# Layer 1's bias goes into the kept x in DRAM, and the layer's end has one sum per tile

## The chip, the cores and the metric

The kernel runs on one core of a Trainium2 chip. The metric is device time in microseconds (us) of one execution, given as the median of the runs; less is better. Before the change it is 2073.58 us (three runs, 2071.27 to 2076.43).

## The reference

Four graph layers stand in a row on one graph of 2708 nodes with 512 features. Each begins with a layer norm and a ReLU, and each adds its result to x. Layer 1, the one that changes, is the only one with a plain bias and no ReLU after its weights:

```python
h = jnp.maximum(_layernorm(x, axis=-1), 0.0)
x = x + _L1_gnn_ref(h, adj, L1_gnn_W, L1_gnn_b)

def _L1_gnn_ref(x, adj, W, b):
    deg = adj.sum(axis=1)
    dis = (deg + EPS) ** (-0.5)
    a_norm = dis[:, None] * adj * dis[None, :]
    h = a_norm @ x
    return h @ W.T + b
```

Layers 0 and 2 end in `relu(aug @ h @ W)` with their own scaling of the adjacency, and layer 3 is two attention-like sums and a sigmoid. All values are float32.

## The kernel before

The 2708 nodes are cut into 22 tiles of up to 128 rows (tiles 0 to 19 are full, 20 and 21 hold the leftovers of the four quarters of the graph). The normalized features `h` of all tiles stay in SBUF. The running x does not: tile t is kept in DRAM as `xs[t]`, 128 by 512 floats, 256 KB.

A layer has two kinds of work.

1. *Products* (`aggregate`). The adjacency times h is done by a two-level scheme of seven products in place of eight. `aggregate` (L668) runs seven outer products in the order 1, 7, 2, 4, 6, 5, 3; each has two column halves u of seven inner products of ten matmuls (L541). For each half SyncE loads four adjacency blocks of 847.5 KB (L445 straight from the input, L447 from sums kept in DRAM) into seven places `obuf`, and VectorE makes the combinations t1, t2, t4 and t3 of them (L512, L513, L514, L516). VectorE also takes the products out of PSUM (L581, L588, L557 to L566). `hooks` may name a function that is traced right after an outer product.
2. *Ends* (`epilogue`, that is `next_x`, L919). Tiles 0 to 9 (H1) are ended before the last outer product 3, tiles 10 to 21 (H2) after it. For each tile: load the kept x (`load_x`, L914, issued by GpSimd, L916); project the aggregated tile through the weights on TensorE (L203, PSUM result `po`); in layer 1 VectorE forms `y = po * dis + b1` (L931), adds y to x (L934); GpSimd stores the new x to `xs[t]` (L935); VectorE takes mean and variance (L234, L235). For every group of three tiles the factors of the norm follow (L224 to L247) and ScalarE writes the new h (L255). In layers 0 and 2 ScalarE makes y with a ReLU in the place of L931. `po` has two PSUM banks, x has seven places, y two.

The bias b1 is fetched once, spread over the 128 partitions, into the place `misc[:, 0:D]` (L963).

The program is traced in order of its text. A planner then orders the instructions of each engine by a simulated time: an instruction stands in its engine's queue where its inputs and its place came free in that simulation, not where the text has it. Inside layer 0 part of the order is written out by hand (`tc.issue_after`); from layer 1 on it isn't. On the chip each queue runs strictly in its order, and all transfers of GpSimd are in one such queue with the waits before them.

Of the kernel before, what the change touches and what calls it, by code (L numbers as in the profile page):

```python
# [10 lines left out]
ALU = mybir.AluOpType  # L11

P = 128
D = 512
# [23 lines left out]
def gnn_kernel(  # L38
# [20 lines left out]
    nc = tc.nc  # L59
# [33 lines left out]
    dinv = dd[:, 1]  # L93
    dis = dd[:, 2]
# [7 lines left out]
    xs = [dram.tile([P, D], FP, name=f"xs{t}") for t in range(NT)]  # L102
# [35 lines left out]
    misc, ends_o = ends[:, ends_o : ends_o + 4 * D], ends_o + 4 * D  # L138
# [7 lines left out]
    def take(places):  # L146

        places.append(places.pop(0))
        return places[-1]

    def new_y():
        return take(y_places)

    def load_w(w):
        w_sb = w_place[:, 0 : NC * D].rearrange("p (c o) -> p c o", c=NC)
        nc.gpsimd.dma_start(w_sb, w.rearrange("(c p) o -> p c o", p=P))
        return w_sb
# [74 lines left out]
    def stats(src, mv):  # L232
        st = small.tile([P, nc.vector.BN_STATS_DIM], FP, tag="st", name="st")
        nc.vector.bn_stats(st, src)  # L234
        nc.vector.bn_aggr(mv, st)  # L235

    def rstd_of(mv, n):
        v = small_cols("rv", n)
        nc.vector.tensor_scalar(v[:, :n], mv[:, :n, 1], LN_EPS, None, ALU.add)
        rstd = small_cols("rstd", n)  # L240
        rsqrt(rstd[:, :n], v[:, :n], n)
        return rstd

    def shift_of(mv, scale, n, at=None):

        b = small_cols("sh", n)
        last = nc.vector.scalar_tensor_tensor(  # L247
            b[:, :n], mv[:, :n, 0], -1.0, scale[:, :n], ALU.mult, ALU.mult
        )
        if at is not None:  # L250
            at.append(last.ins)
        return b

    def normalized(t, src, scale, shift, fs=slice(0, D)):
        nc.scalar.activation(h[:, t, fs], src[:, fs], AF.Relu, bias=shift, scale=scale)  # L255

    def groups(ts):

        res = []
        for t in ts:  # L260
            if res and len(res[-1]) < GT:
                res[-1].append(t)
            else:
                res.append([t])
        return res
# [201 lines left out]
    def by_halves(f, *xs):  # L467

        for ts in (slice(0, KT), slice(KT, 2 * KT)):
            f(*(x[:, ts] for x in xs))  # L470

    def minus_sum(o, a, b):
        nc.vector.scalar_tensor_tensor(o, a, -1.0, b, ALU.mult, ALU.subtract)  # L473
# [45 lines left out]
    def outer_product(p, self_loops, *dests, at=None):  # L519

        X, key, times = OUTER[p]
        with tc.issue_after(at) if at is not None else nullcontext():
            xs_ = inner_x(X)
        if key in PLAIN:
            loops = times if self_loops else 0
        else:
            loops = 0 if self_loops else -times
        for u in range(U):
            blks = [load_o(key, a, b, u) for a, b in QUAD]
            with tc.issue_after(at) if at is not None else nullcontext():  # L530
                ys = inner_y(blks, u, loops)
            multiply(xs_, ys, u, dests)
            free.extend(blks)
# [101 lines left out]
    def tails(self_loops, qs, loaded=None):  # L635


        at = at_pe[-1]
        for n, q in enumerate(qs):
            blk, pieces = loaded[n] if loaded else tail_rows(self_loops, q)  # L640
            for u in range(U):
                tl = pieces[u]
                ps = [
                    (ps_agg if c < NC - 1 else ps_out).tile(
                        [P, W], FP, tag="agg" if c < NC - 1 else "out", name="pt"
                    )
                    for c in range(NC)
                ]
                with tc.issue_after(at) if loaded else nullcontext():
                    tail_products(ps, tl, True)  # L650
                for c in range(NC):
                    d = agg[:, c // 2, q // 2, c % 2, q % 2, u * W : (u + 1) * W]
                    at_end.append(nc.vector.tensor_add(d, d, ps[c]).ins)
            if blk is not None:
                free.append(blk)

    H1 = list(range(0, half))
    H2 = list(range(half, NT))


    def first_part_of_both():
        nc.scalar.copy(agg[:, 0, 1], agg[:, 0, 0])

    def ends_of_sums():
        nc.vector.tensor_add(agg[:, 1, 1], agg[:, 1, 1], agg[:, 0, 1])
        nc.vector.tensor_add(agg[:, 1, 0], agg[:, 1, 0], agg[:, 1, 1])

    def aggregate(self_loops, epilogue, hooks=None):  # L668


        def outer(p, *dests):
            outer_product(p, self_loops, *dests)
            if hooks is not None and p in hooks:
                hooks[p]()

        outer(1, (0, 0, "as it is"))
        first_part_of_both()
        by_halves(nc.vector.tensor_sub, XA, XA, XB)
        outer(7, (1, 1, "as it is"))
        nc.vector.tensor_sub(XB, XB, XD)  # L680
        outer(2, (0, 0, "added"))
        minus_sum(XA, XD, XA)
        nc.vector.tensor_add(XC, XC, XA)
        outer(4, (1, 0, "as it is"))
        tails(self_loops, (0, 1))
        outer(6, (0, 1, "added"))
        ends_of_sums()
        outer(5, (0, 1, "less"), (1, 1, "less"))
        tails(self_loops, (2, 3))
        epilogue(H1)  # L690
        outer(3, (0, 1, "added"))
        epilogue(H2)
# [218 lines left out]
    def project(w_sb, t):  # L911
        return tile_product(t, tile_cols(agg, t), [w_sb[:, c, :] for c in range(NC)])

    def load_x(t, src):  # L914
        xt = take(xt_places)
        nc.gpsimd.dma_start(xt, src[t])  # L916
        return xt

    def next_x(ts, w_sb, scale, bias, src, colscale, after=None):  # L919
        for g in groups(ts):  # L920
            n, t0 = len(g), g[0]
            mv = small.tile([P, KT, 2], FP, tag="mv", name="mv")
            xts = []
            for s, t in enumerate(g):
                xt = load_x(t, src)
                po = project(w_sb, t)
                y = new_y()
                if bias is None:
                    nc.scalar.activation(y, po, AF.Relu, scale=scale[:, t : t + 1])
                else:  # L930
                    nc.vector.scalar_tensor_tensor(  # L931
                        y, po, scale[:, t : t + 1], bias, ALU.mult, ALU.add
                    )
                nc.vector.tensor_add(xt, xt, y)  # L934
                nc.gpsimd.dma_start(xs[t], xt)  # L935
                stats(xt, mv[:, s, :])
                xts.append(xt)
            rstd = rstd_of(mv, n)
            if colscale is not None:
                nc.vector.tensor_mul(rstd[:, :n], rstd[:, :n], colscale[:, t0 : t0 + n])  # L940
            sh = shift_of(mv, rstd, n)
            for s, t in enumerate(g):
                normalized(t, xts[s], rstd[:, s : s + 1], sh[:, s : s + 1])
                if after is not None:
                    after(t)
# [5 lines left out]
    w_sb = []  # L951

    def first_epilogue(ts):
        if not w_sb:
            w_sb.append(load_w(w0))
        next_x(ts, w_sb[0], dinv, None, x, dis)

    first_aggregate(first_epilogue)


    w1_sb = load_w(w1)
    b1_bc = misc[:, 0:D]
    nc.gpsimd.dma_start(b1_bc, b1.partition_broadcast(P))  # L963
    aggregate(False, lambda ts: next_x(ts, w1_sb, dis, b1_bc, xs, dinv))


    def broadcast_columns(po, cs):
# [32 lines left out]
    def h_dots(ts):  # L1000
        for t in ts:
            for k in range(4):
                y = new_y()
                nc.vector.tensor_tensor_reduce(  # L1004
                    y, h[:, t, :], vs[:, k, :], 1.0, 0.0, ALU.mult, ALU.add, hd[:, t, k : k + 1]
                )
            nc.vector.tensor_add(hd[:, t, 2:4], hd[:, t, 2:4], bab)
            nc.vector.tensor_scalar(hd[:, t, 2:4], hd[:, t, 2:4], 0.5, None, ALU.mult)
# [10 lines left out]
    w2_sb = load_w(w2)  # L1019
    vs = None  # L1020

    def make_vs():
# [2 lines left out]

    aggregate(
        True,
        lambda ts: next_x(ts, w2_sb, dinv, None, xs, None, keep_h),
        {2: make_vs, 3: lambda: h_dots((5, 6))},
    )  # L1030

# [442 lines left out]
```

## Time and profile before

The page shows one profiled execution, of 2070.74 us by its own time; the program's instructions span 2069.0 us of it.

| what | us |
|---|---|
| median of the runs | 2073.58 |
| profiled execution | 2070.74 |
| its span | 2069.0 |
| layer 1's first product begins | 450.36 |
| layer 1, end of H1: first and last L931 | 721.03, 752.34 |
| layer 1, end of H2: first and last L931 | 795.36, 834.63 |
| L931, mean of 22 | 0.75 |
| L934 in layer 1, mean of 22 | 0.69 |

Times are from the start of the span. "Idle before, releaser" in a row tells how long the engine waited for that instruction and for what. For a transfer, the time to landing runs from its issue to the last byte's notice.

### The profile page before, as it was taken

How to read it: one execution, taken by the hardware profiler on the slowest of the kernel's cores; microseconds unless marked ns; L12 is line 12 of the kernel's file. 1: busy time of each engine (PE TensorE's matmuls, PEld its weight loads, DVE VectorE, ACT ScalarE, POOL GpSimd, SP SyncE). 2: the span in 40 equal slices, each digit the busy share in tenths (PEclk: the TensorE clock that was granted, in tenths of full speed). 3: DMA queues.
4: the chain of work that ended last, by engine and by line, in shares of the span. 5: the costliest groups of instructions: out<-in, count | busy, mean ns of one | idle time of the engine just before them, and what ended most of it. 6: DMA issues, size and time to landing. Idle time of an engine off the chain costs nothing.

```text
span 2069.0 us, 20285 instructions
## 1 busy us (share of the span) xinstructions
PE 2028.0 (98%) x7330; PEld 1282.2 (62%) x7330; DVE 1495.6 (72%) x2592; ACT 406.2 (20%) x822; POOL 198.8 (10%) x361
## 2 busy tenths in 40 slices
PE   5999999999999999999999999999999999999998
PEld 2566655646666655666664646666677666676666
DVE  4678877756777777766587889967758866677644
ACT  1430001130000010100002130000026444444411
POOL 0111111120000011100002130001001000001011
PEclk9999999999999999999999999999999999999999
DMA  9998595555545444754454565545543332323231
GB/s 369 305 378 265 180 338 187 190 186 179 174 154 176 146 168 142 239 178 161 161 170 144 204 208 188 171 156 186 185 147 121 112 105 95 110 88 123 87 100 52
DMA packets 81476, 363.69 MB, mean 176 GB/s; under 512 B 11568, under 2 KB 16876, under 8 KB 81248
## 3 DMA queue, kind: packets, MB, share of 16 engines
q1 hardware_dynamic: 51104, 245.95, 34.7%
q0 software_dynamic: 30272, 116.45, 17.4%
q8 instruction: 58, 0.95, 0.2%
q14 instruction: 42, 0.34, 0.0%
HBM read 297.39 MB, written 62.19 MB: 174 GB/s over the span
## 4 chain that ended last, share of the span: by engine, by line
PE 83%; DVE 7%; DMA 5%; issue 4%; POOL 1%; ACT 0%; SPq 0%; POOLq 0%; DVEq 0%; ACTq 0%
PE pe L1364 17%; PE pc L541 13%; PE pa L541 13%; PE pd L541 13%; PE po L203 8%; PE pb L541 7%; PE pt L603 3%; DMA obuf<-in_yb_dram 3%; PE pd L1077 1%; PE pc L1077 1%; PE pa L1077 1%; PE pt L608 1%; PE pe L603 1%; DMA osumt<-ends 1%; DVE ends L1004 1%
## 5 line engine op out<-in xcount | busy, mean ns | idle before, releaser
L1364 PE MATMUL pe<-obuf,h 128*128 128x339 f32 x1280 | 373.2, 448 | 0.0
L541 PE MATMUL pa<-obuf,h 128*128 128x339 f32 x1040 | 317.0, 449 | 2.5 <-ACT h L255 1.4
L1364 PEld LDWEIGHTS pe<-obuf,h 128*128 128x128 f32 x1280 | 241.4, 189 | 121.8 <-issue 4.1
L541 PEld LDWEIGHTS pa<-obuf,h 128*128 128x128 f32 x1040 | 195.2, 189 | 109.5 <-issue 9.2
L203 PE MATMUL po<-ends,agg 128*128 128x512 f32 x480 | 207.5, 593 | 0.0
L1228 ACT ACTIVATE e<-r,nsr 128x339 f32<-128x339 f32 x352 | 172.4, 566 | 178.5 <-DVE obuf L1232 86.4
L541 PE MATMUL pb<-t,s 128*128 128x339 f32 x560 | 170.9, 451 | 1.8 <-DVE s L473 1.0
L541 PE MATMUL pc<-t,h 128*128 128x339 f32 x560 | 169.5, 448 | 1.5 <-DVE u L588 1.5
L541 PE MATMUL pd<-t,s 128*128 128x339 f32 x560 | 169.0, 447 | 0.0
L541 PE MATMUL pd<-obuf,s 128*128 128x339 f32 x550 | 166.3, 448 | 0.2 <-DVE agg L562 0.2
L575 ACT COPY v<-pa 128x339 f32<-128x339 f32 x56 | 24.6, 439 | 718.2 <-PE pa L541 691.3
L203 PEld LDWEIGHTS po<-ends,agg 128*128 128x128 f32 x480 | 90.9, 190 | 114.3 <-issue 109.3
L541 PEld LDWEIGHTS pb<-t,s 128*128 128x128 f32 x560 | 106.3, 191 | 57.3 <-DVE t L513 2.1
L541 PEld LDWEIGHTS pc<-t,h 128*128 128x128 f32 x560 | 105.7, 189 | 56.8 <-DVE u L588 3.1
L541 PEld LDWEIGHTS pd<-t,s 128*128 128x128 f32 x560 | 105.8, 189 | 54.1
L541 PEld LDWEIGHTS pd<-obuf,s 128*128 128x128 f32 x550 | 104.0, 189 | 53.9 <-DVE agg L562 1.3
L541 PE MATMUL pc<-obuf,s 128*128 128x339 f32 x450 | 135.9, 448 | 0.0
L541 PEld LDWEIGHTS pc<-obuf,s 128*128 128x128 f32 x450 | 85.1, 189 | 43.8 <-issue 0.5
L935 POOL DMA_DIRECT2D xs<-ends x66 | 35.9, 544 | 780.6 <-DVE ends L934 705.4
L513 DVE TENSOR_TENSOR t<-obuf,t 128x1695 f32<-128x1695 f32 x55 | 105.3, 1915 | 0.0
L1232 DVE SCALAR_TENSOR_TENSOR obuf<-obuf,e 128x1695 f32<-128x1695 f32 x32 | 61.5, 1923 | 57.9 <-DMA obuf<-in_yb_dram 40.7
L514 DVE TENSOR_TENSOR t<-obuf,t 128x1695 f32<-128x1695 f32 x52 | 99.5, 1914 | 0.1
(321 smaller groups left out, 2415.4 us busy)
## 6 DMA issues: line engine op xcount, KB each, us to landing
obuf<-in_yb_dram SPq DMA_DIRECT2D x132, 847.5 KB, 4.5
obuf<-osumt SPq DMA_DIRECT2D x100, 847.5 KB, 4.5
osumt<-obuf POOLq DMA_DIRECT2D x22, 847.5 KB, 12.2
xs<-ends POOLq DMA_DIRECT2D x66, 256.0 KB, 2.3
ends<-xs POOLq DMA_DIRECT2D x60, 256.0 KB, 4.2
obuf<-in_yt_dram SPq DMA_DIRECT2D x28, 339.0 KB, 3.6
obuf<-in_yb_dram POOLq DMA_DIRECT2D x11, 847.5 KB, 11.0
ends<-in_yb_dram SPq DMA_DIRECT2D x9, 847.5 KB, 9.2
```

Source lines behind the costliest of these rows:

```text
L203: nc.tensor.matmul(po, cs[c], ws[c], start=(c == 0), stop=(c == NC - 1))
L513: nc.vector.tensor_add(t2, o22, t1)
L514: at_y.append(nc.vector.tensor_add(t4, o21, t2).ins)
L541: last = nc.tensor.matmul(ps, x[:, k, :], y[:, k, :], start=start and k == 0, stop=k == KT - 1, skip_group_check=not start,)
L575: at_v.append(nc.scalar.copy(v, pa).ins)
L603: nc.tensor.matmul(ps[c], h[:, NF, c * P : (c + 1) * P], tl[:, 0, :], start=start, stop=False)
L608: nc.tensor.matmul(ps[c], h[g, NF + 1, c * P : (c + 1) * P], tl[g, 1, :], start=False, stop=True)
L935: nc.gpsimd.dma_start(xs[t], xt)
L1077: nc.tensor.matmul(ps, xs_[k][:, c], ws[k][:, c], start=start and c == 0, stop=c == 1, skip_group_check=not start,)
L1228: nc.scalar.activation(e[:, k], row, AF.Exp, bias=nsr[:, t, s : s + 1], scale=1.0)
L1232: nc.vector.scalar_tensor_tensor(b, b, 0.0, e1[:, :n], ALU.not_equal, ALU.min)
L1364: nc.tensor.matmul(pe[c], h[:, t, c * P : (c + 1) * P], a, start=(t == 0), stop=False)
```

## The change

The bias leaves `next_x`. In layer 1 one VectorE instruction now makes `x = po * dis + x` in place of two. The bias is added to `xs[t]` in DRAM by 22 accumulating transfers, each of which reads the 2 KB row b1 for all 128 rows of the tile; they are hooked behind the outer products 7, 2, 4 and 6 of layer 1, with tiles 0 to 5, 6 to 11, 12 to 17 and 18 to 21. The fetch of b1 into SBUF goes away. Layers 0 and 2 keep their code under a flag `relu`.

```diff
-    def next_x(ts, w_sb, scale, bias, src, colscale, after=None):
+    def next_x(ts, w_sb, scale, relu, src, colscale, after=None):
...
                 xt = load_x(t, src)
                 po = project(w_sb, t)
-                y = new_y()
-                if bias is None:
+                if relu:
+                    y = new_y()
                     nc.scalar.activation(y, po, AF.Relu, scale=scale[:, t : t + 1])
+                    nc.vector.tensor_add(xt, xt, y)
                 else:
                     nc.vector.scalar_tensor_tensor(
-                        y, po, scale[:, t : t + 1], bias, ALU.mult, ALU.add
+                        xt, po, scale[:, t : t + 1], xt, ALU.mult, ALU.add
                     )
-                nc.vector.tensor_add(xt, xt, y)
                 nc.gpsimd.dma_start(xs[t], xt)
...
     w1_sb = load_w(w1)
-    b1_bc = misc[:, 0:D]
-    nc.gpsimd.dma_start(b1_bc, b1.partition_broadcast(P))
-    aggregate(False, lambda ts: next_x(ts, w1_sb, dis, b1_bc, xs, dinv))
+    def add_b1(ts):
+        for t in ts:
+            nc.gpsimd.dma_start(xs[t], b1.partition_broadcast(P), accum_op=ALU.add)
+
+    aggregate(
+        False,
+        lambda ts: next_x(
+            ts, w1_sb, dis, False, xs, dinv
+        ),
+        {p: lambda k=k: add_b1((H1 + H2)[k * 6 : k * 6 + 6]) for k, p in enumerate((7, 2, 4, 6))},
+    )
```

More of the change, by code (lines that the diff above doesn't have):

```diff
@@ L955, in first_epilogue @@
             w_sb.append(load_w(w0))
-        next_x(ts, w_sb[0], dinv, None, x, dis)
+        next_x(ts, w_sb[0], dinv, True, x, dis)
     first_aggregate(first_epilogue)
     w1_sb = load_w(w1)
-    b1_bc = misc[:, 0:D]
-    nc.gpsimd.dma_start(b1_bc, b1.partition_broadcast(P))
-    aggregate(False, lambda ts: next_x(ts, w1_sb, dis, b1_bc, xs, dinv))
+    def add_b1(ts):
[8 more added lines that the diff above has]
+    )
     def broadcast_columns(po, cs):
@@ L1027, in gnn_kernel @@
         True,
-        lambda ts: next_x(ts, w2_sb, dinv, None, xs, None, keep_h),
+        lambda ts: next_x(ts, w2_sb, dinv, True, xs, None, keep_h),
         {2: make_vs, 3: lambda: h_dots((5, 6))},
```

## The prediction

> **What bounds the kernel now.** I read the page's head first, then the busy times of each engine by stretch, then the order of time in the ends of layer 1 and where layers meet, and last the transfers. The head:
>
> ```profile
> span 2069.0 us, 20285 instructions
> PE 2028.0 (98%) x7330; PEld 1282.2 (62%) x7330; DVE 1495.6 (72%) x2592; ACT 406.2 (20%) x822; POOL 198.8 (10%) x361
> ```
>
> TensorE (PE) has 41 us without work in the whole span; VectorE (DVE) is the second, far behind. An average does not say which is late in layer 1, so here is each engine's busy time by stretch (us of the span, length, then busy time and count of PE, PE's weight loads, DVE, ACT and POOL, the granted clock, the share of the transfer engines and GB/s). The rows are layer 0's end H1 with its last product, layer 0's end H2, layer 1's products, layer 1's end H1, and the start of layer 2:
>
> ```profile
> 330.00:420.00 90.00, 90.00 (x277) 49.14 (x274) 65.05 (x129) 16.75 (x28) 11.42 (x22) 1.00 0.46 158
> 420.00:460.00 40.00, 40.00 (x109) 19.10 (x108) 24.77 (x74) 17.61 (x28) 12.02 (x22) 1.00 0.53 180
> 460.00:720.00 260.00, 260.00 (x946) 168.18 (x945) 186.36 (x249) 9.86 (x18) 1.08 (x2) 1.00 0.51 169
> 717.00:752.00 35.00, 35.00 (x89) 15.50 (x82) 25.24 (x60) 5.06 (x9) 8.15 (x15) 1.00 0.40 137
> 836.00:860.00 24.00, 23.15 (x82) 15.08 (x81) 19.32 (x43) 3.52 (x7) 5.38 (x10) 1.00 0.80 289
> ```
>
> PE is busy without a gap from 330 to 836; only behind the end of layer 1 does it lose 0.85 us. In layer 1's end DVE is busy 25.24 us of 35, and it waits for PE, not the other way round. Two lines of DVE in order of time (start, length, what; in brackets the idle time before and who ended it):
>
> ```profile
> 726.71 0.18 DVE L235 BATCH_NORM_AGGREGATE mv<-st 128x2 f32<-128x6 f32 x1
> 727.90 0.75 DVE L931 SCALAR_TENSOR_TENSOR ends<-po,dd,ends 128x512 f32<-128x512 f32 x1 [1.01 <-PE po L203]
> ```
>
> A tile takes PE 3.43 us there (the L931 of two neighbours begin at 724.47 and 727.90), and DVE is through with it 1.01 us early.
>
> **What goes away.** One L934 per tile of layer 1: 22 of 0.69 us, 15.2 us of DVE. L931 stays at 0.75 us and reads x in place of the bias. As PE never waits in these ends, the worth is between 0 and the 0.85 us that PE loses at 848. What ends late there is this:
>
> ```profile
> 843.81 0.61 DVE L463 SCALAR_TENSOR_TENSOR obuf<-ident,obuf 128x45 f32<-128x45 f32 x3 [2.61 <-DMA obuf<-in_yb_dram]
> 848.01 1.41 PE L541 MATMUL pc<-t,h 128*128 128x339 f32 x4 [0.85 <-DVE u L588]
> ```
>
> DVE itself stood waiting 2.61 us for a block, then did two vector dots (L990, 0.7 us each) ahead of the L588 that PE needed. The dots come that late because their operand was fetched at 836.94, into a y place that the last L934 held until 836.1. Without y in layer 1 the place is free some 2 us earlier, and the dots may fit into the wait. I take half, -0.4 us; bounds -0.85 and 0.
>
> The fetch of b1 (L963, 0.55 us on POOL, landed in 3.7 us, no one waits for it) is worth 0. What hides it is layer 0's long stretch of PE work behind 246.9.
>
> **The moved wait.** L931 now waits for the landing of x; before it was L934, 0.75 us later. Behind it on DVE are the statistics and norms of the group, and PE waits for its PSUM bank. The first seven loads of layer 1 were issued from 438.8 to 462.7, needed from 721 on. Later ones: tile 17's at 808.70, landed in 2.85 us, needed at 819.4. So 0; a load 8 us later would be needed before it costs anything.
>
> **The 22 accumulating transfers.** On POOL the accumulating issues of the trace (L744) take 0.86 us: 22 make 18.9 us, on an engine that worked 1.08 us of the 260 of layer 1's products and 23.4 us of the 130 before. Nothing on PE's path waits for POOL there, so 0. Each add must wait for the landing of its own store of x. In the queue behind it stand further stores, and loads of x that are needed hundreds of us later.
>
> On the transfer engines: an accumulating stream alone in the soft queue q0 (window 150 to 164) and plain block loads in q1 (460 to 720), each with MB and share of 16 engines:
>
> ```profile
> q0 software_dynamic: 384, 2.38, 86.1%
> ...
> q1 hardware_dynamic: 7850, 43.18, 49.8%
> ```
>
> The first is 0.861 x 14 = 12.05 us for 2.38 MB, 5.06 us per MB; the second 129.5 us for 43.18 MB, 3.0. A tile of 0.262 MB costs 0.79 us at the plain rate and 1.33 us accumulating. Those accumulate in SBUF; none in this trace accumulates in DRAM. Below I put the plain 0.79 us, above twice the accumulating price, 2.65 us (destination read and written in DRAM). I take 1.33 us, the same operation. All 22: 29 us, between 17 and 58.
>
> The Trainium skill's page "DMA: Bandwidth & Descriptors", section "Anatomy of one DMA", gives bytes over 436 GB/s beside some 2 us fixed, which would be an estimated 0.6 us of data per tile: it would erase the loss at place A below and leave a sum of -0.4 us. The same page's "Rules for kernel authors" speaks against the change: an accumulate beside another access of the same bytes must wait for the earlier transfer's semaphore; here that is the store of x, landing in 2.3 to 8.7 us.
>
> **When they run.** Not, I think, during layer 1's products. The fetch of b1 stands in the text behind all of layer 0 and was issued at 246.9, some 200 us ahead of layer 1; what has its inputs is put into the queue early. An add needs only its tile's stored x, so I expect tiles 0 to 9 from about 346 to 380 and 10 to 21 from about 419 to 465. The engines are free for 54% of 330:420 (49 us) and 47% of 420:460 (19 us): room for 13 and 16 us. Two places are tight.
>
> *A, the start of layer 1.* In order of time:
>
> ```profile
> 454.37 0.33 SPq L445 DMA_DIRECT2D obuf<-in_yb_dram  x1
> 462.63 1.93 DVE L516 TENSOR_TENSOR obuf<-obuf 128x1695 f32<-128x1695 f32 x1 [3.06 <-DMA obuf<-in_yb_dram]
> 464.48 0.50 DVE L588 TENSOR_TENSOR u<-u,pc 128x339 f32<-128x339 f32 x1
> 465.60 3.02 PE L541 MATMUL pc<-t,h 128*128 128x339 f32 x10
> ```
>
> This block takes 8.2 us, beside the 1 MB of w1, against 4.5 usually. DVE waits 3.06 us for it, L588 is queued behind, and PE's pc at 465.60 needs L588's end at 464.98: slack 0.6 us. The stores of tiles 18 and 19 landed at 447.4 and 450.0, so one or two adds share the engines with the block; those of tiles 20 and 21 cannot start before 460.2 and 462.1. One add in its way is 1.33 - 0.6 = +0.7 us of PE, two +2.1, none 0. I take one. The next blocks (460.08, 462.94) feed work due 10 us later.
>
> *B, layer 0's last product.* A block issued at 374.23 landed at 379.17 and was used from 379.42; the L516 behind it ended at 382.30, and L588 must begin by 384.9 for PE's pc at 385.46: slack 0.25 + 2.6 = 2.9 us. Adds of tiles 7 to 9 fall there; two make 2.7 us, hidden; three +1.1. I take 0.
>
> Sum: -0.4 + 0.7 + 0 = +0.3 us, so 2071.0 for the profiled execution of 2070.74. The median of the runs lies 2.84 us above that execution: 2073.9.
>
> **Rivals.**
>
> 1. *The adds crowd out the blocks.* One mechanism, late blocks at A and B because an accumulate in DRAM costs the upper 2.65 us. It decides once the block of 454.37 lands behind 463.1. For it: the engines' share is 0.90 in 450 to 463, and an accumulating stream is seen at little over half the plain rate. Against: 20 of 22 adds fall where blocks have slack, and a late add 20 also holds back the x loads that share with that block. Price: A, two adds, 5.3 - 0.6 = 4.7; B, three, 8.0 - 2.9 = 5.1; with -0.4, +9.4 us: 2083.0.
> 2. *The adds run where the text has them,* in bursts of six. Each burst is 8 us of the engines on top of a share of 0.51, and one or two blocks come some 4 us late; DVE has pauses of up to 5.3 us per half (before the L581 of 517.30) to take that up. With 0.5 to 1 us lost per burst, +3: 2076.6, not told from no change.
> 3. *DVE was the bound and the whole 15.2 us come back:* 2058.4. For it DVE's 72%; against it every stretch above, with PE idle 0.85 us. Another order from the planner could give a part.
>
> **How the numbers follow.** About 0.3%, 6.2 us, is what can be told from no change. The forecast has 0.56, rival 2 0.08, rival 1 0.30, rival 3 0.06. So slower 0.30, same 0.64, faster 0.06. The range goes from 2070 (the gain of 0.85 and runs low by 2 to 3 us, as the lowest run before was) to 2083.5, just past rival 1; what is left out are a still dearer accumulate and rival 3.
>
> **What would show it.** Right: no L934 in layer 1, L931 still near 0.75 us with idle before it ended by PE, PE gapless from 470 to 836; adds issued from about 346 on, each landing some 3 to 6 us later, with the engines' share up in 330:480. A wrong: the block of about 454 lands later than 463.1 and PE waits for L588 near 466. B wrong: a wait of PE behind 380. The forecast fails if DVE waits for blocks in a stretch where it waited for PE, if an add holds POOL so long that L931 waits for x, or if an add takes far above 2.65 us of the engines.

## The result and the profile after

The changed kernel takes 2088.56 us (median of four runs, 2086.12 to 2092.81), beside 2072.43 us for the kernel before in the same comparison: a ratio of 1.0077, with an interval of 1.0053 to 1.0101. That is 16 us slower, outside the range that was predicted (2070 to 2083.5). The profiled execution took 2090.34 us, its span is 2088.5 us against 2069.0 before. Of all executions behind this document one was slow, a run of E12 below (3061.67 us at a granted clock of 0.655), and E12's median leaves it out.

The head of the page after:

```profile
span 2088.5 us, 20292 instructions
...
PE 2034.5 (97%) x7330; PEld 1286.2 (62%) x7330; DVE 1482.5 (71%) x2570; ACT 405.9 (19%) x822; POOL 218.6 (10%) x382
```

VectorE lost 13 us of work, as the change meant; GpSimd (POOL) got 20 us more. TensorE (PE) has the same 7330 matmuls, and now 54 us without work in place of 41. The same stretches of the clock as before, with the same columns (us of the span, length, busy time and count of PE, PE's weight loads, DVE, ACT, POOL, the granted clock, share of the transfer engines, GB/s), show where:

```profile
330.00:420.00 90.00, 87.58 (x275) 48.08 (x276) 64.07 (x128) 15.27 (x26) 20.08 (x30) 1.00 0.64 183
420.00:460.00 40.00, 37.76 (x94) 16.17 (x92) 20.52 (x62) 14.84 (x23) 13.01 (x20) 1.00 0.50 118
460.00:720.00 260.00, 252.84 (x884) 164.39 (x885) 176.35 (x236) 13.91 (x25) 11.49 (x17) 0.97 0.57 184
717.00:752.00 35.00, 35.00 (x126) 18.48 (x125) 26.04 (x52) 0.20 (x1) 1.64 (x3) 1.00 0.38 132
836.00:860.00 24.00, 24.00 (x72) 11.77 (x71) 14.67 (x42) 8.01 (x13) 8.84 (x16) 1.00 0.59 192
```

In the first three rows PE was busy all the time before; now it lacks 2.42, 2.24 and 7.16 us, and the clock of the third row is 0.97. Nearly all of the loss lies there, in layer 0's ends and the start of layer 1. (By the last two rows the changed kernel is some 20 us behind, so they hold earlier work than before.) In layer 1's own ends, where the text was edited, PE has no gap. Matched by its number in PE's order, a matmul is late by 3.05 us at 279, before the first add has begun, by 5.8 at 382, by 11.84 at 463, 13.6 at 467, 17.6 at 511 and 20.8 at 518; after that no place adds much to it, and 18.65 remain at 1621. The first 3 us come from a stretch at half clock behind a gap of 2.15 us at 274 that both kernels have. E1 below, without any add, has such a stretch too, so it does not come from the adds. All twelve kernels with the single sum have it in their one profile, the two with the old end (before and E2) do not; why is not shown, and E1's runs are level with the kernel before all the same.

The last matmuls before the gaps, and what PE waited for (start, length, what, idle time before it and who ended it):

```profile
382.69 3.13 PE L541 MATMUL pa<-obuf,h 128*128 128x339 f32 x10 [2.42 <-ACT v L575]
...
463.45 2.08 PE L210 MATMUL po<-ends,all_again 128*128 128x512 f32 x2 [5.69 <-ACT ends L208]
...
511.78 6.02 PE L541 MATMUL pb<-t,s 128*128 128x339 f32 x10 [3.70 <-DVE s L473]
```

The first two waits go to ScalarE, but ScalarE had waited too: its copy L208 began at 462.81, after 7.08 us idle for VectorE's L930, the sum of layer 0's ends (L934 before the change). VectorE's lines in order of time say what it lacked:

```profile
374.78 0.69 DVE L930 TENSOR_TENSOR ends<-ends 128x512 f32<-128x512 f32 x1 [6.66 <-DMA ends<-in_x_dram]
...
462.03 0.69 DVE L930 TENSOR_TENSOR ends<-ends 128x512 f32<-128x512 f32 x1 [6.71 <-DMA ends<-in_x_dram]
```

Twice the input x of layer 0 came late. (PE's wait at 511 is another kind: VectorE's L463 at 506.31 had waited 4.14 us for a block, and L473 is queued behind. That block landed 9.8 us after its issue, where its like took 4.3 before, and the engines' share in 470 to 500 is 0.98 in place of 0.51: the late adds, the loads of x and w1 crowd there.) GpSimd's queue shows why x was late (L966 is the add, L935 the store, L916 the load of x):

```profile
361.06 0.86 POOL L966 DMA_DIRECT2D xs<-in_b_dram  x1 [4.69 <-DMA xs<-ends]
361.63 1.41 POOL L935 DMA_DIRECT2D xs<-ends  x2
367.79 0.88 POOL L966 DMA_DIRECT2D xs<-in_b_dram  x1 [4.75 <-DMA xs<-ends]
368.35 1.99 POOL L916 DMA_DIRECT2D ends<-in_x_dram  x3
...
454.74 0.85 POOL L966 DMA_DIRECT2D xs<-in_b_dram  x1 [4.64 <-DMA xs<-ends]
455.30 0.86 POOL L935 DMA_DIRECT2D xs<-ends  x1
455.85 1.41 POOL L916 DMA_DIRECT2D ends<-in_x_dram  x2
```

The planner put each add right behind the store of its tile. On the chip the add must wait until that store has landed, and everything behind it in the queue waits too. The next store then travels behind the add's own packets and lands later (4.6 us after issue in 425 to 436, where no block is loaded; 2.3 alone), so the next add waits longer. A round of store and add takes 6.7 us here (361.06 to 367.79; the two before it 6.0 and 6.1), where PE makes a tile in 3.43 us. GpSimd falls behind, and with it the loads of x for the next tiles of layer 0, which stand in the same queue. The kernel before issued the same loads here:

```profile
358.56 0.54 POOL L916 DMA_DIRECT2D ends<-in_x_dram  x1 [1.10 <-ACT h L255]
...
437.71 1.07 POOL L916 DMA_DIRECT2D ends<-in_x_dram  x2
```

They went out 9.8 us later in the one place and 18.1 us later in the other, where PE's own lateness was some 3 and 6 us. The adds wait for stores 17 times, 76.3 us in all, and land 4.6 to 12.3 us after issue (median 5.8).

With two of the gaps came a stretch of 6.8 us in which the clock was halved (the same columns as above):

```profile
460.00:466.80 6.80, 3.35 (x5) 1.85 (x6) 2.08 (x4) 1.27 (x2) 2.26 (x3) 0.50 0.68 180
...
511.20:518.00 6.80, 6.22 (x11) 3.87 (x12) 4.83 (x5) 2.66 (x2) 0.00 (x0) 0.50 0.07 28
```

By the matched matmuls these stretches cost 1.7 and 3.2 us on top of the gaps. So of the 19.5 us between the two spans some 3 are of the stretch at 274, 9.8 of the two gaps for x with their half clock, and 6.9 of the gap at 511 with its own.

### The profile page after: what moved, and what is told of

It reads as the page before. It is cut to its first block, busy times and chain, and to the rows that moved or that the text cites. A ratio compares the mean times of both kernels' runs of the same rounds, so it can differ in the third digit from the quotient of the medians.

```text
span 2088.5 us, 20292 instructions
## 1 busy us (share of the span) xinstructions
PE 2034.5 (97%) x7330; PEld 1286.2 (62%) x7330; DVE 1482.5 (71%) x2570; ACT 405.9 (19%) x822; POOL 218.6 (10%) x382
## 4 chain that ended last, share of the span: by engine, by line
PE 78%; issue 11%; DVE 5%; DMA 4%; POOL 2%; ACT 0%; SPq 0%; POOLq 0%; DVEq 0%; ACTq 0%
PE pe L1374 17%; PE pa L541 13%; PE pc L541 13%; PE pd L541 12%; PE po L203 7%; PE pb L541 7%; PE pt L603 3%; DMA obuf<-in_yb_dram 2%; PE pe L603 1%; PE pt L608 1%; DMA obuf<-osumt 1%; PE pc L1087 1%; PE pd L1087 1%; PE pa L1087 1%; DMA ends<-in_x_dram 1%
## 5 line engine op out<-in xcount | busy, mean ns | idle before, releaser
L935 POOL DMA_DIRECT2D xs<-ends x66 | 41.9, 668 | 695.2 <-DVE ends L930 327.1
L541 PEld LDWEIGHTS pc<-obuf,s 128*128 128x128 f32 x450 | 85.1, 189 | 43.8 <-issue 0.5
L513 DVE TENSOR_TENSOR t<-obuf,t 128x1695 f32<-128x1695 f32 x55 | 105.3, 1915 | 0.0
L512 DVE TENSOR_TENSOR t<-obuf 128x1695 f32<-128x1695 f32 x48 | 92.1, 1918 | 10.8 <-DMA obuf<-osumt 6.6
```

The source lines that it names most:

```text
L512: nc.vector.tensor_add(t1, o12, o11)
L513: nc.vector.tensor_add(t2, o22, t1)
L541: last = nc.tensor.matmul(ps, x[:, k, :], y[:, k, :], start=start and k == 0, stop=k == KT - 1, skip_group_check=not start,)
```

## The experiments

Three theories stood at the start. *P*: the edited end and the order that the planner makes of it lose the time. *Q*: GpSimd's queue does, in which adds hold up layer 0's loads and stores. *C*: the adds' time on the transfer engines does, as it crowds out blocks and loads. Line numbers shift by a few between kernels.

| run | us (median) | before | ratio and interval |
|---|---|---|---|
| E1 no adds | 2072.13 | 2072.16 | 0.9999 [0.9990, 1.0007] |
| E2 adds alone | 2090.57 | 2072.16 | 1.0089 [1.0074, 1.0105] |
| E3 adds held, bursts of six | 2090.78 | 2072.16 | 1.0091 [1.0076, 1.0105] |
| E4 early adds, a quarter of the bytes | 2076.78 | 2072.16 | 1.0016 [1.0003, 1.0029] |
| E5 adds held, pairs | 2086.07 | 2072.92 | 1.0064 [1.0050, 1.0077] |
| E6 loads of x on SyncE | 2089.37 | 2072.92 | 1.0075 [1.0062, 1.0087] |
| E7 bursts, a quarter of the bytes | 2075.23 | 2072.92 | 1.0009 [1.0000, 1.0018] |
| E8 early adds, bias read from SBUF | 2077.66 | 2072.92 | 1.0024 [1.0015, 1.0032] |
| E9 bursts of plain writes | 2079.29 | 2072.32 | 1.0030 [1.0020, 1.0039] |
| E10 pairs, bias read from SBUF | 2076.40 | 2072.32 | 1.0020 [1.0011, 1.0030] |
| E11 layer 0's ends on ScalarE's queue | 2077.55 | 2072.32 | 1.0024 [1.0013, 1.0034] |
| E12 the same without adds | 2076.09 | 2074.07 | 1.0012 [1.0000, 1.0024] |

### E1 and E2: each half of the change by itself

E1 keeps the single sum and drops the hooks, so that the bias is left out; E2 keeps the two instructions of before and adds the hooks, so that it is added twice.

```diff
# E1, from the changed kernel
         lambda ts: next_x(
             ts, w1_sb, dis, False, xs, dinv
         ),
-        {p: lambda k=k: add_b1((H1 + H2)[k * 6 : k * 6 + 6]) for k, p in enumerate((7, 2, 4, 6))},
# E2, from the kernel before
+    def add_b1(ts):
+        for t in ts:
+            nc.gpsimd.dma_start(xs[t], b1.partition_broadcast(P), accum_op=ALU.add)
...
         lambda ts: next_x(ts, w1_sb, dis, b1_bc, xs, dinv),
+        {p: lambda k=k: add_b1((H1 + H2)[k * 6 : k * 6 + 6]) for k, p in enumerate((7, 2, 4, 6))},
```

> The changed kernel without its 22 accumulating transfers (layer 1's bias is left out); the one sum per tile stays. Theory Q (each add waits in GpSimd's queue for its tile's store, and the stores and x loads queued behind it come late): with no adds the whole loss of 16 us goes, 2071 to 2073 us, ratio to before 0.9990 to 1.0010, no wait of VectorE for x loads in layer 0's ends, full clock near 460 and 511 us. Theory C (the adds take the transfer engines from the block loads): the same time. Theory P (the edited end and the planner's other order cost time by themselves): at least 5 us of the loss stays, 2077 us or more. The half-clock stretch near 272 us that the changed kernel's profile has and the one before has not: if it is there again, it doesn't come from the adds.

> The kernel before with the 22 accumulating transfers put beside its old end of layer 1 (the bias is added twice). Theories Q and C: the loss is in the adds alone, 2085 to 2092 us. Theory P: 2078 us or less.

E1 is the time before to 0.1%: the shorter end is worth nothing that can be measured, and it costs nothing either. P falls. E2 has the whole loss, with PE's waits in the same three places (4.9 us at L210, 3.8 at pb, 2.9 at pa) and VectorE waiting 13.2 us in two waits for layer 0's x. The loss is in the adds.

### E3: the adds at the place where the text has them

The six adds of a hook stand behind a one-column GpSimd copy that reads the last result of the outer product, so they cannot be issued earlier.

```diff
-    def add_b1(ts):
-        for t in ts:
-            nc.gpsimd.dma_start(xs[t], b1.partition_broadcast(P), accum_op=ALU.add)
+    mark = const.tile([P, 4], FP, name="mark")
+    def add_b1(ts, k, d):
+        held = nc.gpsimd.tensor_copy(mark[:, k : k + 1], d[:, 2 * W - 1 : 2 * W])
+        with tc.issue_after(held.ins):
+            for t in ts:
+                nc.gpsimd.dma_start(xs[t], b1.partition_broadcast(P), accum_op=ALU.add)
...
```

> The changed kernel, but each six adds are held back behind a one-column copy on GpSimd that reads the last result of their outer product, so that they really run during layer 1's products. Theory Q: no store or x load of layer 0 stands behind an add any more; 2070 to 2076 us. Theory C: the same 22 x 1.4 us of the transfer engines now fall in bursts of six on the block loads of layer 1, VectorE waits for blocks and TensorE for VectorE; 2079 us or more.

Layer 0's ends have no late x any more, and the loss is as large as ever: PE stalls of 4.41, 1.89 and 4.65 us at 573, 617 and 656, each with half clock around it. The third, PE and then VectorE before it:

```profile
656.16 5.60 PE L541 MATMUL pc<-t,h 128*128 128x339 f32 x10 [4.65 <-DVE u L588]
```

```profile
652.83 0.61 DVE L463 SCALAR_TENSOR_TENSOR obuf<-ident,obuf 128x45 f32<-128x45 f32 x3 [4.87 <-DMA obuf<-osumt]
```

Q cannot make such a wait for a block; C can, and E7 tests it. The second burst, in the row of its stretch (the kernel before, then E3) and in E3's GpSimd transfers there (packets, MB, share of 16 engines):

```profile
585.00:613.00 28.00, 28.00 (x99) 18.55 (x98) 18.27 (x23) 0.88 (x2) 0.00 (x0) 1.00 0.40 130
```

```profile
585.00:613.00 28.00, 28.00 (x99) 18.54 (x98) 11.89 (x18) 1.32 (x3) 5.97 (x8) 1.00 0.95 233
```

```profile
q0 software_dynamic: 944, 1.84, 44.2%
```

With 1.84 MB from GpSimd the share is 0.95 in place of 0.40, and the six adds land in 15.3 us (median): 44.2% of 28 us are 12.4 us for six adds and one load of x. Taking 0.8 us off for the load (the plain price of the prediction), an add holds all engines for 1.9 us. VectorE starves first (11.89 us of work in place of 18.27), and PE a few us later, behind the stretch: the stall at 617. So moving the adds away from layer 0 trades one mechanism for the other.

### E4 and E7: a quarter of the bytes

E4 is the changed kernel, and E7 is E3, with adds of 128 of the 512 columns.

```diff
-            nc.gpsimd.dma_start(xs[t], b1.partition_broadcast(P), accum_op=ALU.add)
+            nc.gpsimd.dma_start(
+                xs[t][:, 0:P], b1[0:P].partition_broadcast(P), accum_op=ALU.add
+            )
```

> The changed kernel with adds of 128 of the 512 columns (three quarters of the bias are left out): a quarter of the bytes, the same number of transfers and waits, at the same places. Theory Q: an add still waits for its store and is waited for by later stores, each some 4 us instead of 5.1 to land; most of the loss stays, 2080 to 2086 us. Theory C: a quarter of the loss, 2074 to 2077 us.

> The held bursts of six again, at the text's place behind outer products 7, 2, 4 and 6, but each add takes 128 of 512 columns; three quarters of the bias are left out. The number of transfers, their waits and their order on GpSimd are those of the held bursts (2090.8 us, 19 us lost). Theory C (engine time of the bytes, crowding): a burst is a quarter as long and the loss falls to a third or less: 2073 to 2079 us, with block loads landing in under 8 us. If the count of transfers or of packets is what costs (each add is still 128 rows): 2083 us or more.

E7 settles C for the bursts: the same transfers, waits and order, a quarter of the bytes, and 2.3 us lost in place of 18.6. It is the bytes, not the number of transfers. E4 lands in C's band, but it does not tell C from Q: its adds land in 4.4 us (median) in place of 5.8, so GpSimd's queue kept up as well, and VectorE waited for no x.

### E9: plain writes in place of adds

The bursts of E3, with the same source and place.

```diff
# E9, from E3
-                nc.gpsimd.dma_start(xs[t], b1.partition_broadcast(P), accum_op=ALU.add)
+                nc.gpsimd.dma_start(xs[t], b1.partition_broadcast(P))
```

> The held bursts of six (2090.8 us, 19 us lost) with the same rows and the same place, but as plain writes: the bias overwrites the kept x and is not added, so the output is not that of the reference. Theory A (it is the accumulation that makes the transfer dear: 2048 B packets of 178 to 266 ns against 4096 B packets of 159 ns for plain ones): engine time per transfer falls from 1.4 to 2.1 us to under 1 us, the bursts are half as long, and the loss falls to half or less: 2073 to 2082 us. Theory B (any 256 KB transfers set together between the block loads cost so much, or the 128-fold read of one row does): 2085 us or more.

The loss falls from 18.6 to 7.0 us, as A has it. GpSimd's transfers in the stretch of the second burst, where E3 has 44.2%:

```profile
q0 software_dynamic: 538, 1.75, 28.3%
```

28.3% of 28 us are 7.9 us in place of 12.4, and less the 0.8 us for the load of x 1.25 us per transfer (1.75 MB are the load and 5.7 transfers) in place of 1.9. Over all four bursts the difference is smaller. GpSimd's transfers in 470 to 720, E3 first, then E9:

```profile
q0 software_dynamic: 3728, 7.60, 19.7%
```

```profile
q0 software_dynamic: 2320, 7.60, 16.7%
```

Less 5.5 us for the seven loads of x, an add took 2.0 us of all engines and a write 1.65 (a quarter add of E7, by its 12.2%, 1.1). So A's time came true, but not A's figure of under 1 us, and the loss (18.6, 7.0 and 2.3 us) falls much faster than the engines' time. E9 changes two things, as the plain writes also go in half as many packets; against the number of packets as the cause stands E7, which kept it. The 1.25 to 1.65 us are above the plain price of 0.79 that I had as lower bound; whether the source, one row read for all 128, or the company of the blocks makes that difference, this run does not tell.

### E5 and E10: pairs, and where the bias is read

Two adds behind each of eleven halves, held as in E3; E10 reads the bias from a copy in SBUF.

```diff
# E5, from the changed kernel; half is called at the end of each column half
...
+    def add_b1(d):
+        if to_add:
+            k = len(to_add) // 2
+            held = nc.gpsimd.tensor_copy(mark[:, k : k + 1], d)
+            with tc.issue_after(held.ins):
+                for t in (to_add.pop(0), to_add.pop(0)):
+                    nc.gpsimd.dma_start(xs[t], b1.partition_broadcast(P), accum_op=ALU.add)
...
# E10, from E5
+    b1_bc = misc[:, 0:D]
+    nc.gpsimd.dma_start(b1_bc, b1.partition_broadcast(P))
...
-                    nc.gpsimd.dma_start(xs[t], b1.partition_broadcast(P), accum_op=ALU.add)
+                    nc.gpsimd.dma_start(xs[t], b1_bc, accum_op=ALU.add)
```

> The 22 adds two at a time, one pair behind each of the eleven halves of outer products 1, 7, 2, 4, 6 and 5 of layer 1; each pair stands in GpSimd's queue behind a one-column copy of the last result of its half, so that it can't run earlier. Theory C (an add costs the time that its packets crowd blocks out of the transfer engines, and only where several stand together): two adds are some 3 to 4 us of engine time in a half of some 23 us whose engines are half free, so each is hidden: 2071 to 2077 us, with blocks landing in at most 8 us and no wait of PE over 1 us in layer 1's products. Theory C2 (each add costs engine time wherever it falls, as the blocks are due as soon as they can land): near the held bursts, 2082 us or more. Theory Q (GpSimd's queue holds up the x loads of layer 0) also expects 2071 to 2077 here, as layer 0 is left alone: this kernel tells C from C2, not from Q.

> The adds two at a time behind each half (2086.1 us, some 13 us lost), reading the bias from a copy in SBUF in place of the row in DRAM. The engine time of an add is the same by its packets (median 178 ns either way), but its packets came within 2.2 us in place of 3.1. Theory C2 (the engine time is what the blocks lose): 2083 to 2088 us. Theory R (how long an add keeps single engines behind the others counts, as a block waits for its last engine): half of the loss or more comes back, 2073 to 2080 us, with blocks landing near 4.6 us.

E5 missed what I expected of C: even two adds in a half cost, 13 us in all. Between 470 and 720 PE lacks 6.96 us, in five stalls of 1.0 to 1.6 us at pc and pd, with DVE waiting up to 5.3 us for a block; another of 2.61 us with half clock behind it follows at 862 (E1, without adds, waits 1.80 there). I had treated the engines' free half as room to hide in, but a block has its due time, and what stands beside it delays it. E10 gives most of it back. The GpSimd queue of both in 470 to 720, E5 first, then E10:

```profile
q0 software_dynamic: 3728, 7.60, 21.0%
```

```profile
q0 software_dynamic: 3728, 7.60, 17.5%
```

The 250 us of the window times the share are 52.5 and 43.8 us. Less 5.5 us for the seven loads of x, an add takes 2.1 us of all engines with the row in DRAM and 1.7 us with SBUF, and lands in 6.5 us (median) in place of 8.5. The expectation that the engine time stays the same did not hold under load; that the reading decides did.

### E8: the early adds read from SBUF

The source of the changed kernel's adds is changed as in E10; all else stays.

> The changed kernel, with the bias fetched once into SBUF, spread over 128 partitions, and all 22 adds reading it there in place of the 2 KB row in DRAM. Theory R (what makes an add slow is 128 readers of the same 2 KB row): packets go from 178 ns toward the 100 ns or so of a plain one of that size, adds land in under 4 us, and the kernel comes to 2082 us or less. Theory A (the read and write at the destination in DRAM are what is slow): packets and landings as they were (178 ns, 4.6 to 5.8 us), and 2085 to 2092 us.

11 of the 16 us came back, though not by the way expected. The packets are as slow as they were (median 178 ns for 2048 bytes), and all 22 adds take as much of the 16 engines (42.5 us; 41.7 in the changed kernel). What changed is the landing (the add's transfers from issue to landing, first the changed kernel, then E8):

```profile
DMA to landing us min/median/max: 4.6/5.8/12.3
```

```profile
DMA to landing us min/median/max: 4.0/4.3/10.7
```

A round of store and add takes some 5.2 us in place of 6, GpSimd falls less behind, and VectorE waits less for layer 0's x (us, times, longest; the changed kernel first, then E8):

```profile
DVE ends L930 <- DMA ends<-in_x_dram: 13.4, 2, 6.7
```

```profile
DVE ends L930 <- DMA ends<-in_x_dram: 4.8, 2, 3.0
```

PE's wait at L210 shrinks from 5.7 to 0.9 us, and the one at 511 is gone. With the bytes and packets unchanged, this speaks for Q in layer 0's ends. E8 changes two things at once, the memory that is read and that 128 rows read the same 2 KB; which of them makes the difference stays open.

### E6, E11 and E12: GpSimd's queue set free

E6 moves layer 0's loads of x to SyncE, E11 loads and stores to ScalarE, E12 is E11 without the adds.

```diff
# E6
-        nc.gpsimd.dma_start(xt, src[t])
+        (nc.sync if src is x else nc.gpsimd).dma_start(xt, src[t])
# E11 and E12
-        nc.gpsimd.dma_start(xt, src[t])
+        (nc.scalar if src is x else nc.gpsimd).dma_start(xt, src[t])
...
-                nc.gpsimd.dma_start(xs[t], xt)
+                (nc.scalar if src is x else nc.gpsimd).dma_start(xs[t], xt)
```

> The changed kernel, with layer 0's loads of x (L916) issued on SyncE's queue in place of GpSimd's; the adds stay on GpSimd, early. Theory Q (an add that waits for its store, and lands in 5 to 6 us, holds the loads of x queued behind it on GpSimd): VectorE's two waits of 6.66 and 6.71 us at L930 for x vanish, PE gets the 2.75 and 6.0 us near 382 and 463 back and with them the stretch of half clock at 460 (1.3 us): 2077 to 2081 us, leaving the stall near 511 if the first blocks of layer 1 are still late. Theory C (the adds' bytes crowd out the loads themselves): the x loads land as late as before, on whatever queue they are: 2086 or more.

> The changed kernel, with both the loads of x and the stores of layer 0's ends issued on ScalarE's queue; GpSimd has the adds, and layer 1's loads behind them. The adds still run early and have the same bytes. Theory Q (GpSimd's queue, in which an add stands between a tile's store and the next tiles' stores and loads): no wait of VectorE at L930 for x over 1 us, the 2.75 and 6.0 us near 382 and 463 come back, 2073 to 2081 us; the rest, if any, at layer 1's first blocks near 511. Theory C (the adds' bytes alone): the stalls near 382 and 463 stay, 2085 us or more. Should ScalarE's own queue be held by the stores' waits, PE would wait for L929's ReLU and the run says nothing between the two.

> The control for the run with layer 0's ends on ScalarE's queue (2077.6 us): the same kernel without the adds (the bias is left out). If the queue of these transfers by itself is worth nothing without adds, as all theories here have it, this comes to the time before, 2070 to 2075 us, and the 5 us between are the adds' bytes and landings that are left. If ScalarE's queue by itself speeds or slows layer 0 (below 2068 or above 2077 us), the other run's 11 us were not only GpSimd's queue set free.

E6 missed Q's figure. The waits for x did vanish, but the wait only moved. What SyncE's own queue waited for most in 340 to 420 (us, times, longest):

```profile
SPq L916 <- DMA xs<-ends: 45.0, 7, 9.7
```

A load of x needs the place of an earlier tile, which is free once that tile's store has landed. The stores still stood on GpSimd behind adds, so the loads stood on SyncE for 45 us in all, with the blocks of the products behind them, and PE waited for want of one (PE, then VectorE before it):

```profile
401.64 3.76 PE L541 MATMUL pc<-t,h 128*128 128x339 f32 x6 [11.57 <-DVE u L588]
```

```profile
398.31 0.61 DVE L463 SCALAR_TENSOR_TENSOR obuf<-ident,obuf 128x45 f32<-128x45 f32 x3 [14.35 <-DMA obuf<-in_yb_dram]
```

E11 moves the stores too, and there the theory holds: no wait of VectorE for x, no stall at 382 or 463, and 11 us back. Stores and loads there stand neither behind a waiting add nor in one transfer queue with its packets; E11 does not part the two. What is left of the adds' stalls is one at the start of layer 1 (PE, then VectorE before it):

```profile
471.53 4.75 PE L541 MATMUL pc<-t,h 128*128 128x339 f32 x10 [2.41 <-DVE u L588]
```

```profile
469.13 1.93 DVE L516 TENSOR_TENSOR obuf<-obuf 128x1695 f32<-128x1695 f32 x1 [5.64 <-DMA obuf<-in_yb_dram]
```

That block landed in 11.3 us (8.2 before), beside four adds, w1 and the loads of x. E12, the control, has no stall there and is 2 us over the kernel before, with an interval that begins at no change; so ScalarE's queue is no gain by itself, and of E11's 5.2 us up to half may be the queue's and the rest the adds'.

No version here beats the kernel before, and by E1 none of this kind would by more than 0.1%: with no adds at all it is level.

## Why the prediction was wrong

- **What goes away** (-0.4): its size is too small to tell, and E1 shows no difference that can be measured. The way to it was wrong: PE's wait for L588 behind layer 1 is still there, 0.72 us at 867.71 in the changed kernel and 1.80 at 849.69 in E1 (0.85 at 848.01 before). The dots did not fit into VectorE's wait for the block; in E1 they run behind it, from 846.08.
- **The moved wait** (0): right. In layer 1's ends L932 (L931 before) waited for x in two cases of 1.7 us, and PE in none.
- **The 22 accumulating transfers**: the step that failed. It said "Nothing on PE's path waits for POOL there, so 0" and that behind an add stand "loads of x that are needed hundreds of us later". That holds for layer 1's seven loads, not for layer 0's own, which stand between the adds because the adds come early. The profile of before had the row: L916 at 358.56 and 437.71, in the very stretches that I had named for the adds. I had worked out that an add waits for its store and would land in 3 to 6 us, and did not set that round against PE's 3.43 us per tile. What came in its place: a round of some 6 us, two waits of VectorE for x (13.4 us), and two gaps of PE (2.42 and 5.69 us). E11 and E8 show the price: 11 of the 16 us go when the queue is free or its round shorter. The text named a neighbour of it as a way to fail (a held POOL, and L931 waiting for x in layer 1's ends), and gave it no price.
- **The price on the engines**, 1.33 us with bounds 0.79 and 2.65: at its packets' median an add took 1.42 us (128 packets of 178 ns on 16 engines), over the 22 of the changed kernel 1.9 on the mean, and up to 2.1 beside blocks (E5). Inside the bounds, but the value was the undisturbed one, in stretches that are not empty.
- **When they run**: right for the first (348.93; 346 was forecast) and the landing's median (5.8 us), wrong for the last: 489.38 in place of 465, since each waits for the one before it.
- **Place B** (0): right; the wait at 382 is late x, not the block of place B.
- **Place A** (+0.7): the changed kernel was late there already, and its stall came at 511, when adds, loads of x and the 1 MB of w1 had all slid into layer 1's first blocks. E11 shows place A by itself: 2.41 us of wait and 1.7 of half clock. Rival 1's 4.7 was nearer.
- **Rival 1** (2083.0) had the sign and one mechanism of two. **Rival 2** put a burst of six at "8 us of the engines" and +3 in all; E3 shows 12 us of them, one burst spread over 587 to 610, and +18.6. **Rival 3** falls with E1.
- **Not in any term**: that a PE stall costs more than its length. Half clock at the two gaps made 4.9 us of what the changed kernel lost (1.7 and 3.2).

## What to carry to other kernels

A transfer that must wait for another is priced by its queue: list every instruction behind it, work out the round (wait, issue, landing), and set it against the time in which the main engine makes one tile. Moving work off an engine that was not the bound bought nothing (E1), while the transfers that take its place must fit between loads that have due times; half of the transfer engines free on average was no room to hide in (E5). Where such a wait moves to another queue, follow the place that it holds, too: E6 made the stall twice as long.

## What the runs showed of the hardware

- An accumulating transfer into DRAM is slow per byte: packets of 2048 bytes in 178 ns are 11.5 GB/s per engine, beside 25.8 for plain ones of 4096 bytes in 159 ns. Plain packets of the same 2048 bytes, which layer 0's loads and stores have on SyncE's and ScalarE's queues (E6, E11, E12), take 84 ns, less than half. Beside blocks the difference shrinks: 2.0 us of the engines for an add in E3, 1.65 for a plain write in E9.
- With the bias in DRAM an add landed in 4.4 us at the least after its issue (E6; 4.6 in the changed kernel), with the bias in SBUF in 3.8 (E10). The Trainium skill's page "DMA: Bandwidth & Descriptors", section "Anatomy of one DMA", would put a 256 KB transfer at an estimated 2.6 us. The plain stores and loads of x come near it at their quickest (2.3 and 2.8 us in the kernel before), the adds do not, and the measurement decides.
- The clock was halved at gaps of PE, for 3.4 or 6.8 us (13.7 in E6). In the fourteen traces, between 240 and 1300 us, by PE's idle time as in the rows above, none of 22 gaps from 1.05 to 1.81 us went with it, 19 of 31 from 1.84 to 3.24 us did, and all 7 from 3.70 us up. The Trainium skill's page "TensorE: Matmul & The Clock Gate", section "Why this matters for your kernels", warns of idle gaps over some 3 us; here a gap of 1.87 us was enough at times (E10).
